# Proj of batch two with four block products split in seven, its activation sums issued one product ahead, and the last chunk of each first product last

## The chip, the cores and the metric

The kernel runs on one core of one Trainium2 chip. The metric is the device time of one execution in microseconds, taken as the median over runs. A profile of one further execution shows what each engine did: TensorE (PE, with its weight loads shown as PEld), VectorE (DVE), ScalarE (ACT), GpSimd (POOL) and SyncE (SP), whose queue issues most of the transfers.

## The reference

One transformer block with cross attention, in float32: four batches (B = 4), 512 rows each, model width D = 512, 16 heads, inner width 2048.

```
q = layer_norm(x, ln1) @ q_w + q_b ; k, v = ctx @ k_w + k_b, ctx @ v_w + v_b
attn = softmax(mask(q k^T / sqrt(32))) ; hidden = (attn v) @ cproj_w + cproj_b + x
y = gelu(layer_norm(hidden, ln2) @ fc_w + fc_b)        # 512 x 2048, "fc"
out = hidden + y @ proj_w + proj_b                     # 512 x 512, "proj"
```

The change is in proj of the last three batches, numbered 1, 2 and 3. "Batch two" is `b == B - 2`, "batch three" is `b == B - 1`, and batch one is `b == SPLIT`.

## The kernel before, in words

Attention of all batches comes first, with the MLP of batch zero and half of that of batch one woven into it. From `att.close()` on, `last_mlps` (line 590) does the rest: the second half of batch one, then batches two and three whole, each as an fc stage and a proj stage. Instructions are issued in the order of the program on each engine (`manual_schedule`); buffers come from pools, and a tile that needs a buffer waits until its last user has let it go. PSUM holds eight banks here: four buffers "acc" (`acc_half`, `acc_tile`) and four "half" (`half_tile`).

**Seven products for eight.** A product of 2 x 2 blocks is done with seven block products in the manner of Strassen and Winograd. Both operands need sums first: of the left side s1 to s4, of the right side t1 to t4 (some written in place over a block that is no longer needed). The seven products are assembled with a few additions (u2, u3).

- fc, by pairs of inner chunks (`fc_seven`, line 483): a pair is seven products of 128x128 weights with 256 columns. `sum_wa(c)` makes the sums of the weights of pair c on DVE, four operations of 256 columns, one pair ahead. ACT applies the gelu to each half of the pair (line 513), into `ga[:, c]`. `g_sums(c)` forms the sums of the activations of two chunks, four DVE operations of 512 columns, into `gs` and over `g21`. After the last chunk, `g_sums(NP - 2)` runs.
- proj (`project`, line 670): seven block products `q1` to `q7` of the activations g11 to g22 (with sums s1 to s4) by the weights b11 to b22 (with t1 to t4). The inner dimension is 8 chunks (`pairs`; 4 in batch one, whose other half was done before). A plain block product (`product`, line 676) is 2 x 8 matmuls of 128x128 by 256 columns; the trace has two records for each float32 matmul, so 32 records (16 in batch one). `q1` runs over t = 0 and then t = 1, each with chunks from first to last.
- A block product can itself be split in seven (`forty_nine`, line 627): 28 matmuls of 128 columns, 56 records, in the order r1, r26 (its two halves), r57, r34. It needs sums of its own on both sides. `x_sums(x, free)` (line 620) makes those of the activations: three DVE operations and one on POOL, 512 columns each, written over three quarters of the matrix `free` that is no longer read; the second is called s2 here. `w_sums(i, w)` makes those of the weights: four DVE operations of 512 columns. These 20 operations for five weight matrices lie in a list, `to_split`, and a table, `splits`, says how many are taken from it at each chunk of the fc stages of batches two and three. The first 16 records of a `forty_nine` (r1 and half of r26) need no sums; the 17th needs s2 and t2. Each `forty_nine` ends in four DVE additions from PSUM, placed in the program at the end of the call's products.

Before the change batch one splits no block product, batch two splits `q7` and `q5`, and batch three splits `q2`, `q3`, `q6`, `q7` and `q5`; `q1` and `q4` are plain everywhere. In batch two the `x_sums` of a split product stand directly ahead of it in the program (lines 734 and 737); in batch three they stand one product ahead (lines 699, 700, 706, 709, 712).

**What stands around the products.** `sums()` loads the next batch's rows (`load_hid`, SP transfers, then a bias addition on POOL, line 357). `turns()` transposes the next batch's normed rows on PE (line 159, four PSUM tiles) and ACT and DVE move them to `yT` (lines 164 and 162, two each). `join(engine, i, j, src)` adds a finished block to the residual rows, in two operations of 256 columns on DVE or POOL. `store` writes out through SP. `middle()` makes `y_sums` and the weight sums of chunk 0 for the next batch on DVE, ahead of the fourth product.

Of the kernel before, what the change touches and what calls it, by code (L numbers as in the profile page):

```python
# [20 lines left out]
P = 128  # L21
B, L, D, H = 4, 512, 512, 16
# [12 lines left out]
SPLIT = 1  # L35
# [17 lines left out]
def xattn_block(ctx: ExitStack, tc: tile.TileContext, x, encT, mask, q_w, k_w, v_w, c_w, fc_w, p_w, vecs, rows, out):  # L53
    nc = tc.nc
# [32 lines left out]
    pb = pbt.rearrange("p (c i n) -> p c i n", c=NF // 2, i=2)  # L87
    pt = ptt.rearrange("p (s c n) -> p s c n", s=3, c=NF // 2)
# [360 lines left out]
    HL = L // 2  # L449
# [4 lines left out]
    def add(engine, o, x0, x1):  # L454
        engine.tensor_tensor(o, x0, x1, ALU.add)  # L455
# [24 lines left out]
    def acc_half(name):  # L480
        return acc_tile(name).rearrange("p (i l) -> p i l", i=2)
# [108 lines left out]
    def last_mlps():  # L590
# [21 lines left out]
        def w_sums(i, w):  # L612
            w11, w12, w21, w22 = quarters(w)
            t1, t2, t4 = more(i)
            return [lambda o=o, x=x, y=y: sub(o, x, y) for o, x, y in (
                (t1, w12, w11), (t2, w22, t1), (w12, w22, w12), (t4, w21, t2)
            )]

        def x_sums(x, free):
            x11, x21, x12, x22 = quarters(x)  # L620
            s1, s2, s4 = free if isinstance(free, list) else quarters(free)[:3]
            add(nc.vector, s1, x21, x22)
            sub(s2, s1, x11)
            sub(x21, x11, x21)
            sub(s4, x12, s2, nc.gpsimd)
# [31 lines left out]
        def half_tile(name):  # L657
            return ps_last.tile([P, 2, HL], F32, tag="half", name=name)
# [11 lines left out]
        def project(b, pairs, sums, turns, middle):  # L670
            g11, g12, g21, g22 = (ga[:, :, k, j * HL : (j + 1) * HL] for j in range(2) for k in range(2))
            b11, b12, b21, b22 = (pb[:, :, k, j * HL : (j + 1) * HL] for k in range(2) for j in range(2))
            t1, t2, t3, t4 = pt[:, 0], pt[:, 1], b12, pt[:, 2]
            s1, s2, s3, s4 = gs[:, 0], gs[:, 1], g21, gs[:, 2]

            def product(o, a, w, ts_=range(2)):
                for t in ts_:
                    for c in pairs:
                        nc.tensor.matmul(  # L679
                            o[:, t], a[:, c, ts(t, P)], w[:, c], start=(c == pairs[0]), stop=(c == pairs[-1])  # L680
                        )

            def hid(i, j, t):
                return S["hid", b, 2 * i + t][:, j * HL : (j + 1) * HL]

            def join(engine, i, j, src):
                for t in range(2):
                    add(engine, hid(i, j, t), src[:, t], hid(i, j, t))

            def store(i, j):  # L690
                for t in range(2):
                    nc.sync.dma_start(out=out[b, ts(2 * i + t, P), j * HL : (j + 1) * HL], in_=hid(i, j, t))

            q1 = acc_half(f"q1p_{b}")
            product(q1, g11, b11)
            nc.scalar.copy(p1p, q1)
            sums()
            if b == B - 1:
                x_sums(g12, x_more)
                x_sums(s4, g11)  # L700
                forty_nine(b, "2", u3p, g12, b21, x_more, 4)
                turns()
                join(nc.gpsimd, 0, 0, p1p)
                join(nc.gpsimd, 0, 0, u3p)
                store(0, 0)
                x_sums(s2, g12)
                forty_nine(b, "3", u3p, s4, b22, g11, 0)
                join(nc.gpsimd, 0, 1, u3p)
                x_sums(s3, s4)
                forty_nine(b, "6", u2p, s2, t2, g12, 1)  # L710
                add(nc.vector, u2p, u2p, p1p)
                x_sums(s1, s2)
                forty_nine(b, "7", u3p, s3, t3, s4, 2)
                add(nc.vector, u3p, u3p, u2p)
                for i, j, src in ((0, 1, u2p), (1, 0, u3p), (1, 1, u3p)):
                    join(nc.gpsimd, i, j, src)
                forty_nine(b, "5", p1p, s1, t1, s2, 3)
                join(nc.vector, 0, 1, p1p)
                join(nc.vector, 1, 1, p1p)
            else:  # L720
                q2 = acc_half(f"q2p_{b}")
                product(q2, g12, b21)
                turns()
                q3 = half_tile(f"q3p_{b}")
                product(q3, s4, b22)
                join(nc.vector, 0, 0, q2)
                join(nc.gpsimd, 0, 0, p1p)
                store(0, 0)
                q6 = acc_half(f"q6p_{b}")
                product(q6, s2, t2)  # L730
                add(nc.vector, u2p, q6, p1p)
                join(nc.vector, 0, 1, q3)
                if b > SPLIT:
                    x_sums(s3, g11)
                    forty_nine(b, "7", u3p, s3, t3, g11, 2)
                    add(nc.vector, u3p, u3p, u2p)
                    x_sums(s1, g12)
                else:
                    q7 = half_tile(f"q7p_{b}")
                    product(q7, s3, t3)  # L740
                    add(nc.vector, u3p, q7, u2p)
                for i, j, src in ((0, 1, u2p), (1, 0, u3p), (1, 1, u3p)):
                    join(nc.gpsimd, i, j, src)
                if b > SPLIT:
                    forty_nine(b, "5", p1p, s1, t1, g12, 3)
                    q5 = p1p
                else:
                    q5 = half_tile(f"q5p_{b}")
                    product(q5, s1, t1)
                join(nc.vector, 0, 1, q5)  # L750
                join(nc.vector, 1, 1, q5)
            store(0, 1)
            store(1, 1)
            middle()
            q4 = half_tile(f"q4p_{b}"), acc_half(f"q4p_{b}")
            for t in range(2):
                product(q4[t], g22, t4, (t,))
                add(nc.vector, hid(1, 0, t), q4[t][:, t], hid(1, 0, t))
                nc.sync.dma_start(out=out[b, ts(2 + t, P), :HL], in_=hid(1, 0, t))
# [3 lines left out]
        half = FIRST * FQ // 2  # L763
        to_split = (
            w_sums(2, pb[:, :, 0, HL:]) + w_sums(3, pt[:, 0])
            + w_sums(4, pb[:, :, 1, :HL]) + w_sums(0, pb[:, :, 1, HL:]) + w_sums(1, pt[:, 1])
        )
        splits = {
            (B - 2, 1): 2, (B - 2, 3): 2, (B - 2, 5): 2, (B - 2, 7): 2,
            (B - 1, 0): 2, (B - 1, 1): 3, (B - 1, 3): 3, (B - 1, 5): 2, (B - 1, 7): 2,  # L770
        }
        for b, pairs, new in (
            (SPLIT, range(half, NP), range(half)), (SPLIT + 1, range(NP), ()), (SPLIT + 2, range(NP), ())
        ):
            for c in pairs:

                def sums(b=b, c=c):
                    if c + 1 < NP:
                        sum_wa(c + 1)
                    for _ in range(splits.get((b, c), 0)):  # L780
                        to_split.pop(0)()

                fc_pair(b, c, sums)
                if c + 2 < NP:
                    load_wa(c + 2)
                elif b + 1 < B:
                    load_wa(c + 2 - NP)
                if new:
                    n = (c - half + 2) % half
                    for i in range(2):  # L790
                        nc.sync.dma_start(out=pb[:, n, i, :], in_=p_w[ts(2 * n + i, P), :])
                if c % 2 == 0 and c != pairs[0]:
                    g_sums(c - 2)

                if b == B - 3 and c < NP - 1:
                    stat2(B - 1, c - pairs[0])
                if b == B - 2:
                    if c == 0:
                        stat2(b + 1, NT - 1)
                        ln_rs((2, b + 1))  # L800
                    for t in {4: (0,), 5: (1, 2), 7: (3,)}.get(c, ()):
                        norm2(b + 1, t)
            g_sums(NP - 2)

            def sums(b=b, new=new):
                for c in new[::2]:
                    p_sums(c)
                if b + 1 < B:
                    load_hid(b + 1, range(NT))

            def turns(b=b):
                if b + 1 < B:
                    run(turns2(b + 1))
                if b == SPLIT:
                    load_xn(B - 1)

            def middle(b=b):
                if b + 1 < B:
                    y_sums(b + 1)
                    sum_wa(0)  # L820

            project(b, pairs, sums, turns, middle)


# [260 lines left out]
```

## Time and profile before

| what | value |
|---|---|
| median of 3 runs | 802.93 us (801.81 to 803.38) |
| the profiled execution, its own time | 804.41 us |
| its span, first to last instruction | 802.6 us |
| mean granted clock of TensorE | 0.996 |
| fc of batch two, PE's start to start | 603.91 to 652.53 us |
| proj of batch two | 652.53 to 705.02 us |
| fc of batch three | 705.02 to 753.37 us |
| proj of batch three, to the end | 753.37 to 802.6 us |
| DVE busy in proj of batch two (652.5 to 705) | 26.48 us |
| POOL busy in the same stretch | 14.62 us |

The profile numbers lines of the kernel as L495. A timeline line gives the start, the length, engine, line, operation, output and inputs, the shape and the count of merged records, and in brackets the time that the engine sat idle before it and what ended that. PE's matmuls are pipelined, so the length of a group reaches a little into the next one; the distance between the starts of two groups is the better measure. L642 is the matmul of `forty_nine`, L679 that of `product`, L495 that of the fc; L455 is any `add`, L452 any `sub`, told apart by their tiles.

### The profile page before, as it was taken

The numbers are of one execution on the slowest core, as the hardware profiler recorded it, in microseconds if no ns is written. First come the engines' busy times: TensorE is split into PE (matmuls) and PEld (weight loads), VectorE is DVE, ScalarE is ACT, GpSimd is POOL, SyncE is SP. The second block draws the span as 40 slices with busy tenths as digits, with TensorE's granted clock in tenths as the row PEclk, the third lists the DMA queues.
The fourth block names the chain that finished last, engine by engine and source line by source line (L and its number), as shares of the span: only waits on it lengthen the run. The fifth ranks groups of instructions, "written<-read, shape, count | busy, mean of one in ns | idle before, by whom it ended". The sixth has DMA issues, their size and how long they took to land.

```text
span 802.6 us, 12542 instructions
## 1 busy us (share of the span) xinstructions
PE 783.1 (98%) x4346; PEld 500.8 (62%) x4346; DVE 614.4 (77%) x1244; ACT 341.3 (43%) x752; POOL 139.7 (17%) x157
## 2 busy tenths in 40 slices
PE   9999999989999999999999999999999999999998
PEld 6545455456655555556553333446888888888897
DVE  3789998878889867779877988536878991689873
ACT  2567765537763545547553479500201220012200
POOL 1110030055121041001131100020050020300052
PEclk9999999989999999999999999999999999999999
DMA  8899998947896887787778799873523230022001
GB/s 324 289 238 229 234 237 244 233 110 176 209 242 179 222 217 183 175 195 215 178 161 219 196 261 256 202 248 105 186 102 105 82 115 14 26 80 79 14 15 40
DMA packets 60959, 137.19 MB, mean 171 GB/s; under 512 B 12464, under 2 KB 15664, under 8 KB 60768
## 3 DMA queue, kind: packets, MB, share of 16 engines
q1 hardware_dynamic: 59472, 132.43, 60.8%
q0 software_dynamic: 896, 2.82, 1.1%
q10 hardware_dynamic: 528, 1.14, 0.7%
q8 instruction: 35, 0.57, 0.3%
q14 instruction: 28, 0.23, 0.1%
HBM read 58.22 MB, written 6.82 MB: 81 GB/s over the span
## 4 chain that ended last, share of the span: by engine, by line
PE 79%; DVE 13%; SPq 3%; ACT 2%; issue 2%; DMA 1%; POOL 0%; DVEq 0%; POOLq 0%; ACTq 0%
PE q L495 13%; PE accp L554 8%; PE sc L262 7%; PE av L345 7%; PE accc L386 7%; PE accv L240 7%; PE acck L218 6%; PE r L642 5%; PE accq L228 5%; DVE ga L455 4%; PE accf L536 3%; DVE ptt L266 3%; SPq L328 2%; PE q4p L679 2%; PE tp L159 1%
## 5 line engine op out<-in xcount | busy, mean ns | idle before, releaser
L270 ACT ACTIVATE ptt<-ptt,mn 128x512 f32<-128x512 f32 x256 | 181.6, 711 | 137.1 <-DVE mn L266 136.8
L266 DVE CUSTOM_DVE_ANT_0 ptt<-sc,mb 128x512 f32<-128x512 f32 x256 | 161.0, 685 | 34.0 <-PE sc L262 33.8
L285 DVE STREAM_TRANSPOSE tb<-ptt 128x1024 f32<-128x1024 f32 x96 | 119.2, 1242 | 14.4 <-ACT ptt L270 14.1
L554 PE MATMUL accp<-pbt,gt 128*128 128x512 f32 x192 | 86.7, 600 | 0.0
L495 PE MATMUL q<-yT,gt 128*128 128x256 f32 x320 | 78.9, 379 | 0.0
L262 PE MATMUL sc<-pbt 32*128 32x512 f32 x512 | 73.6, 645 | 4.7 <-DVE mn L266 2.5
L513 ACT ACTIVATE ga<-ga,vec 128x512 f32<-128x512 f32 x40 | 26.7, 714 | 97.8 <-DVE ga L455 97.8
L495 PEld LDWEIGHTS q<-yT,gt 128*128 128x128 f32 x320 | 60.8, 190 | 8.7 <-issue 0.5
L554 PEld LDWEIGHTS accp<-pbt,gt 128*128 128x128 f32 x192 | 35.2, 190 | 49.0 <-issue 46.0
L240 PEld LDWEIGHTS accv<-ptt,xe 128*128 128x128 f32 x512 | 58.6, 192 | 9.7 <-issue 6.3
L495 PE MATMUL q<-ys,gt 128*128 128x256 f32 x240 | 61.8, 380 | 0.5 <-DVE ys L452 0.5
L240 PE MATMUL accv<-ptt,xe 128*128 128x128 f32 x512 | 60.9, 277 | 0.0
L218 PE MATMUL acck<-xe,ptt 128*128 128x512 f32 x128 | 59.2, 603 | 0.0
L228 PE MATMUL accq<-xe,ptt 128*128 128x512 f32 x128 | 58.4, 599 | 0.0
L386 PE MATMUL accc<-wc,oT 128*128 128x512 f32 x128 | 56.6, 596 | 0.0
L345 PE MATMUL av<-pT,v 128*32 128x256 f32 x768 | 48.1, 392 | 2.9 <-ACT ptt L270 0.8
L252 POOL TENSOR_TENSOR v<-v,row 128x512 f32<-128x512 f32 x16 | 20.4, 1274 | 173.6 <-ACT v L245 173.6
L495 PEld LDWEIGHTS q<-ys,gt 128*128 128x128 f32 x240 | 45.4, 190 | 7.4 <-DVE ys L452 0.9
L270 ACT ACTIVATION_READ_ACCUMULATOR ptt<-ptt,mn 128x1 f32 x256 | 47.8, 187 | 0.0
L262 PEld LDWEIGHTS sc<-pbt 32*128 32x128 f32 x512 | 20.2, 184 | 37.9 <-issue 21.5
L228 PEld LDWEIGHTS accq<-xe,ptt 128*128 128x128 f32 x128 | 23.6, 190 | 32.4 <-issue 30.4
L386 PEld LDWEIGHTS accc<-wc,oT 128*128 128x128 f32 x128 | 23.8, 190 | 31.5 <-issue 29.8
(183 smaller groups left out, 1125.3 us busy)
## 6 DMA issues: line engine op xcount, KB each, us to landing
pT<-tb SPq DMA_DIRECT2D x384, 136.0 KB, 2.4
pbt<-p_w_dram SPq DMA_DIRECT2D x40, 256.0 KB, 3.1
gt<-fc_w_dram SPq DMA_DIRECT2D x40, 256.0 KB, 2.6
gt<-tb SPq DMA_DIRECT2D x64, 136.0 KB, 2.7
xe<-tb SPq DMA_DIRECT2D x56, 136.0 KB, 3.1
pbt<-fc_w_dram SPq DMA_DIRECT2D x24, 256.0 KB, 3.8
ptt<-k_w_dram SPq DMA_DIRECT2D x16, 256.0 KB, 3.9
xe<-encT_dram SPq DMA_DIRECT2D x16, 256.0 KB, 4.9
```

The costliest lines, as they stand in the source:

```text
L218: nc.tensor.matmul(acc, S["wk", w][:, d, :], eT[:, d, :], start=(d == 0), stop=(d == ND - 1))
L228: nc.tensor.matmul(acc, S["wq", w][:, d, :], xT[:, d, :], start=(d == 0), stop=(d == ND - 1))
L240: nc.tensor.matmul(acc[:, ts(t, P)], eT[:, d, ts(t, P)], S["wv", w][:, d, :], start=(d == 0), stop=(d == ND - 1),)
L262: nc.tensor.matmul(sc[:, h, :], qT[r, ts(qt, P)], kT[r, :], start=True, stop=True)
L266: nc.vector.tensor_tensor_reduce(out=s, in0=sc[:, h, :], in1=S["mb", w // NG], scale=1.0, scalar=FMAX, op0=ALU.add, op1=ALU.min, accum_out=mn,
L270: nc.scalar.activation(s, s, AF.Exp, bias=mn, scale=-1.0, accum_out=sums[:, qt, h : h + 1])
L285: nc.vector.transpose(*two_heads[k])
L345: nc.tensor.matmul(av[ts(h, HD), : 2 * P].rearrange(shape, **kw), v[:, t, ts(h, HD)], p[t][h], start=(t == 0), stop=(t == NT - 1),)
L386: nc.tensor.matmul(acc, S["oT", b][:, g, ts(t, P)], wc[:, g, :], start=(g == 0), stop=(g == NG - 1))
L495: nc.tensor.matmul(o, x[:, k], y[:, k], start=(k == 0), stop=(k == 1))
L554: nc.tensor.matmul(acc, gT[q % 2][:, k, ts(t, P)], S["pw", b, q * FQ + k], start=(k == 0), stop=(k == FQ - 1))
L642: nc.tensor.matmul(r, x[:, c], w[:, c], start=(c == 0), stop=(c == NP // 2 - 1))
```

## The change

`q1` is written out: all chunks but the last, for t = 0 and then t = 1, and then the last chunk for both. In batch two `q2` stays plain, and `q3`, `q6`, `q7` and `q5` are split, with the `x_sums` of each one product ahead, as in batch three; `q3` and `q6` were plain there. The join of `q2` in batch two stays on DVE and stands after POOL's join of `p1p` on the same rows. The weight sums are reordered (b21's last) and redistributed: before, 8 in the fc of batch two and 12 in the fc of batch three; after, 8 in the fc of batch two (2, 3 and 3 at chunks 1, 3 and 5), 8 in proj of batch two (4 ahead of the sums for `q3`, 4 ahead of `q3` itself) and 4 in the fc of batch three (2 at chunks 1 and 3). The branch that `b > SPLIT` took before is now taken by batch one alone, with plain products, as it had them.

```diff
             q1 = acc_half(f"q1p_{b}")
-            product(q1, g11, b11)
+            steps = [(t, c) for c_ in (pairs[:-1], pairs[-1:]) for t in range(2) for c in c_]
+            for n, (t, c) in enumerate(steps):
+                nc.tensor.matmul(
+                    q1[:, t], g11[:, c, ts(t, P)], b11[:, c],
+                    start=n == 0, stop=c == pairs[-1], skip_group_check=t > 0,
+                )
             nc.scalar.copy(p1p, q1)
             sums()
-            if b == B - 1:
-                x_sums(g12, x_more)
+            if b > SPLIT:
+                if b == B - 1:
+                    x_sums(g12, x_more)
+                else:
+                    split(4)
                 x_sums(s4, g11)
-                forty_nine(b, "2", u3p, g12, b21, x_more, 4)
+                if b == B - 1:
+                    forty_nine(b, "2", u3p, g12, b21, x_more, 4)
+                    q2 = u3p
+                else:
+                    q2 = acc_half(f"q2p_{b}")
+                    product(q2, g12, b21)
                 turns()
                 join(nc.gpsimd, 0, 0, p1p)
-                join(nc.gpsimd, 0, 0, u3p)
+                join(nc.gpsimd if b == B - 1 else nc.vector, 0, 0, q2)
                 store(0, 0)
                 x_sums(s2, g12)
+                if b < B - 1:
+                    split(4)
                 forty_nine(b, "3", u3p, s4, b22, g11, 0)
...
-                if b > SPLIT:
-                    x_sums(s3, g11)
-                    forty_nine(b, "7", u3p, s3, t3, g11, 2)
-                    add(nc.vector, u3p, u3p, u2p)
-                    x_sums(s1, g12)
-                else:
-                    q7 = half_tile(f"q7p_{b}")
-                    product(q7, s3, t3)
-                    add(nc.vector, u3p, q7, u2p)
+                q7 = half_tile(f"q7p_{b}")
+                product(q7, s3, t3)
+                add(nc.vector, u3p, q7, u2p)
...
-                if b > SPLIT:
-                    forty_nine(b, "5", p1p, s1, t1, g12, 3)
-                    q5 = p1p
-                else:
-                    q5 = half_tile(f"q5p_{b}")
-                    product(q5, s1, t1)
+                q5 = half_tile(f"q5p_{b}")
+                product(q5, s1, t1)
...
-            + w_sums(4, pb[:, :, 1, :HL]) + w_sums(0, pb[:, :, 1, HL:]) + w_sums(1, pt[:, 1])
+            + w_sums(0, pb[:, :, 1, HL:]) + w_sums(1, pt[:, 1]) + w_sums(4, pb[:, :, 1, :HL])
...
-        splits = {
-            (B - 2, 1): 2, (B - 2, 3): 2, (B - 2, 5): 2, (B - 2, 7): 2,
-            (B - 1, 0): 2, (B - 1, 1): 3, (B - 1, 3): 3, (B - 1, 5): 2, (B - 1, 7): 2,
-        }
+        splits = {(B - 2, 1): 2, (B - 2, 3): 3, (B - 2, 5): 3, (B - 1, 1): 2, (B - 1, 3): 2}
+
+        def split(n):
+            for _ in range(n):
+                to_split.pop(0)()
```

In the fc stages the loop that took the sums from the list now calls `split(splits.get((b, c), 0))`.

## Prediction

> **What bounds the kernel now.** I read the page's busy table first, then the TensorE (PE) row of the timeline through the stage that the change touches, then the waits of PE there.
>
> ```profile
> span 802.6 us, 12542 instructions
> PE 783.1 (98%) x4346; PEld 500.8 (62%) x4346; DVE 614.4 (77%) x1244; ACT 341.3 (43%) x752; POOL 139.7 (17%) x157
> ```
>
> PE is the bound as an average; what the change can win is PE work or gaps between PE groups in its own stage. The timeline of PE gives the start of each group, so the distance between two starts, set against the same group elsewhere, shows each gap.
>
> ```profile
> 652.53 3.18 PE L679 MATMUL q1p<-pbt,ga 128*128 128x256 f32 x14
> 656.56 4.15 PE L679 MATMUL q1p<-pbt,ga 128*128 128x256 f32 x18 [0.84 <-ACT ga L513]
> 660.55 7.07 PE L679 MATMUL q2p<-pbt,ga 128*128 128x256 f32 x32
> 667.45 2.13 PE L159 MATMUL tp<-ident,hn 128*128 128x128 f32 x16
> 669.42 7.07 PE L679 MATMUL q3p<-pbt,gs 128*128 128x256 f32 x32
> 676.33 7.07 PE L679 MATMUL q6p<-ptt,gs 128*128 128x256 f32 x32
> 683.23 1.95 PE L642 MATMUL r<-pbt,ga 128*128 128x128 f32 x16
> 686.24 1.16 PE L642 MATMUL r<-tt,ga 128*128 128x128 f32 x8 [1.06 <-DVE ga L452]
> ...
> 690.81 1.95 PE L642 MATMUL r<-ptt,gs 128*128 128x128 f32 x16
> 693.54 1.16 PE L642 MATMUL r<-tt,ga 128*128 128x128 f32 x8 [0.79 <-DVE ga L452]
> ...
> 698.11 2.11 PE L679 MATMUL q4p<-ptt,ga 128*128 128x256 f32 x9
> ```
>
> This is proj of batch two. A plain block product takes 676.33 - 669.42 = 6.91 us (32 records of 0.216). Three gaps stand in the row: the first product waits for ScalarE's last gelu, and both seven-way products (7, then 5) wait after their first 16 records for VectorE (DVE) to form the activation sums. What a seven-way product takes with its sums ready stands in batch three:
>
> ```profile
> 761.06 1.95 PE L642 MATMUL r<-pbt,ga 128*128 128x128 f32 x16
> 767.31 1.95 PE L642 MATMUL r<-pbt,gs 128*128 128x128 f32 x16
> 773.57 1.95 PE L642 MATMUL r<-ptt,gs 128*128 128x128 f32 x16
> ```
>
> 767.31 - 761.06 = 6.25 us, 56 records of 0.1116. In the stages around it (fc of batch two, 603.91 to 652.53, and of batch three, 705.02 to 753.37) groups follow each other without a bracket: PE paces them, although DVE runs there almost without a pause.
>
> **Part 1: the last chunk of each first product goes last.** Batch two: start to start 660.55 - 652.53 = 8.02, against 6.91 for a plain product: 1.11 lost. Batch three: 761.06 - 753.37 = 7.69, 0.78 lost. Batch one (16 records, 3.45): 576.99 to 581.23 = 4.24, 0.79 lost. In the new order PE reaches the last chunk after 28 of 32 records: 652.53 + 28 x 0.216 = 658.6, while the gelu it needs ended at 656.5; batch three 759.4 against 757.0; batch one, after 12 of 16, 579.6 against 578.9. All three waits go: **2.68 us**. What is late next? The second product reads the last chunk's other half, ready with the second gelu 0.6 us later, long before. In batch three the second product needs its s2 at 753.37 + 6.91 + 16 x 0.1116 = 762.07; DVE finished it at 761.74 already, and the eight splits taken from DVE in that fc let the last gelu end about 2 us earlier (DVE then waits for PE's 753.4 and one 0.69 add, not for its backlog). In batch one DVE is late with its p_sums until 591.6 whatever PE does, but PE's third product needs only the chunk sums, ended at 582.3. No loss.
>
> **Part 2: products 3 and 6 become seven-way.** Each removes 6.91 and adds 6.25: 2 x 0.66 = **1.31 us** of PE. Second (plain both before and after), 7 and 5 (seven-way both) keep theirs.
>
> **Part 3: sums one product ahead.** Gaps now: 683.23 + 16 x 0.1116 = 685.02 against 686.24, 1.22; 690.81 + 1.79 = 692.60 against 693.54, 0.94. Together **2.16 us**, if the new sums are on time. That has to be followed on DVE's queue, which gains two x_sums (six 128x512 operations at a pitch of about 0.65), two seven-way assemblies (four adds, 1.55 each) and eight weight splits (pitch 0.65), about 12 us in all, and loses two splits before and two 0.37 us joins. GpSimd (POOL) gains two subtractions of 1.6 and two joins of 0.71. On the old clock, with PE at 652.53 + 6.91 + 6.91 + 1.97 for the transposes, product 3 starts at 668.3:
>
> - The chunk sums end at 663.05 as now (they run beside POOL's four bias adds, see below). Four splits: 665.65. x_sums for product 3: s2 at 666.95, last at 667.6. PE wants s2 at 668.3 + 1.79 = 670.1. Slack 3.1 us.
> - The two yT evacuations (0.76 each) then run 667.6 to 669.1. Product 3 needs two PSUM buffers at 668.3 and 669.2, which the transposes have just held: lost 0 if they are ScalarE's or the first of DVE's, at worst 2.0 if one is the second product's, whose join now stands behind POOL's join. it can't gain, as PE has the transposes to end first. 0.2 taken: the first DVE evacuation ends at 668.4, ScalarE's second at about 669.3.
> - The join of the second product moved behind POOL's p1p join on the same elements: POOL subtracts 667.0 to 668.6, joins to 670.0; DVE, stopped by that, ends at 670.4. Behind it in DVE's queue stand the x_sums for product 6: s2 at 671.7; then the splits it needs: t2 at about 674.75 with one slowed operation. PE wants both at 668.3 + 6.25 + 1.79 = 676.35. Slack 1.6; bounds of the wait 0 and 2, 0.2 taken (nearest row: batch three, where the same chain waits nowhere).
> - For product 7: assemblies of 3 end 677.6, s2 at 678.9, wanted at 682.6. For 5: wanted at 688.9, ready near 683.5. No wait.
>
> **Cover of the moved splits.** The fc of batch two keeps eight, one each later in chunks 3 and 5 and none in 7. DVE falls up to 1.0 us further behind at chunk 6 and is level at 7. Weight sums of chunk 7, ended at 646.5, become 647.5; PE uses the third of them at 648.21: cost 0. Without that cover it would be at most the 1.0. The fourth product, joins and y_sums follow at the old distances, since POOL's last joins (from 688.2, six of 0.71) end at 692.5, before product 5 does (693.3). SP's queue keeps its order: load_hid still follows the first product, and no transfer is added or moved past another.
>
> **The rule that speaks against it.** POOL and DVE get in each other's way in this trace:
>
> ```profile
> 657.84 4.66 POOL L357 TENSOR_TENSOR hid<-hid,row 128x512 f32<-128x512 f32 x3 [0.36 <-DMA hid<-xa]
> 658.06 1.64 DVE L452 TENSOR_TENSOR ga<-ga 128x512 f32<-128x512 f32 x1
> 659.62 1.75 DVE L452 TENSOR_TENSOR gs<-gs,ga 128x512 f32<-128x512 f32 x1
> 661.41 1.64 DVE L452 TENSOR_TENSOR gs<-ga,gs 128x512 f32<-128x512 f32 x1
> ```
>
> The same DVE form takes 0.69 alone, 1.64 to 1.75 here: a pitch of 1.68 against 0.65, 1.03 lost an operation. From the gelu's end (656.95) to t2 of product 6 DVE has 16 such operations and 2.4 us of others: 669.75 unslowed. POOL works about 10 us in that stretch, so at most 6 of the 16 are slowed: 675.9, still inside 676.35. The Trainium skill ("SBUF — State Buffer", section "Who interferes with whom") says that a DVE instruction with two SBUF inputs fully blocks until a GpSimd one that reads SBUF has finished. By that rule to the letter each of the six would wait the whole 1.56 of a POOL instruction, PE would wait 2.8 us for product 6, and the gain would be 3.4. The rows show 1.03, and I go by them.
>
> **The sum.** 2.68 + 1.31 + 2.16 = 6.15, less 0.4 for new waits: **5.75 us**. The profiled execution took 804.41 (span 802.6, 1.8 around it): 798.66 by the sum. The median of the runs is 802.93, 1.48 below the profiled one, so the median forecast is 802.93 - 5.75 = **797.2**.
>
> **Rivals.**
> - A, DVE is late in batch two: the sums or PSUM buffers of products 3 and 6 come 2 to 5 us late (worst bounds 2.0 and 2.0, and more POOL overlap). For: DVE's added 12 us fall into 41 us (it was busy 26.5 of 52.5 there), and the early part is crowded. Against: the slacks above. 799 to 802; 0.17, of which 0.13 stays over 0.2% faster.
> - B, the first products gain nothing: the wait for the last chunk only moves (to the second product, or PE's next sums). Then 2.68 goes: 799.9. For: DVE and ScalarE end the chunk as late as before in batches one and two. Against: the last gelu leads by 0.7 to 2.4 us. 0.06.
> - C, slower: DVE becomes the bound of batch two's proj through POOL. All 16 operations slowed would put t2 at 686.2, 9.9 late: 806.7. It decides from 12.4 slowed operations of 16, where the loss eats 6.15; POOL's work covers 6. 0.03.
> - That the change does not do what it says (sums issued ahead but held until the product before has finished reading) is in A: each x_sums overwrites only a matrix whose product is done by then (the first product ends at 659.5, the second at 666.4).
>
> **How the numbers follow.** Forecast (new waits of 0 to 1.5) 0.74, A 0.17, B 0.06, C 0.03. Low end: no new wait, 796.8, less 0.8 for the scatter of the runs (801.81 to 803.38): 796.0. High end, both worst bounds of A with no other gain lost, 6.15 - 4.0 = 2.15 would be 800.8; 800.0 leaves out about 0.13. About 0.2% (1.6 us) is what a measurement of this kernel can tell from no change: faster than 801.3 is the forecast, B and 0.13 of A, 0.93; same 0.04; slower 0.03.
>
> **What would show it.** In the changed profile: no bracket on any q1p row, and q1p of batch two 6.91 from its start to q2p's; four seven-way products of 6.25 with no bracket after their first 16 records; q4p of batch two 4.2 to 4.6 us nearer to the end of its fc; the two fc still 48.4 to 48.6 long. Wrong would be: a bracket on product 3's first records (PSUM buffer), on its 17th (sums late) or product 6's (splits late), or a gap in fc of batch two after chunk 5.

## The result and the profile after

The changed kernel takes 798.08 us (median of 6 runs, 796.44 to 800.61) against 802.79 for the kernel before beside it (6 runs, 801.81 to 803.98): ratio 0.9944, 95% interval 0.9925 to 0.9962. The same kernel once more, in another comparison: 797.0 against 803.03, ratio 0.9927 (0.9911 to 0.9944). The forecast was 797.2, a ratio of 0.9929 to the 802.93 it started from. The profiled execution took 797.57.

The page's head after:

```profile
span 795.4 us, 12670 instructions
PE 779.7 (98%) x4394; PEld 502.0 (63%) x4394; DVE 622.0 (78%) x1256; ACT 341.9 (43%) x754; POOL 145.4 (18%) x161
```

The span is 7.2 us shorter, but 0.93 of that lies in code that is the same in both: batch one's first product starts at 576.06 instead of 576.99. Over all 14 profiles of this document that start varies from 573.65 to 577.60 us. So I compare stages within a profile, from the start of batch one's first product on ("the tail": 225.61 us before, 219.34 after, 6.27 less). PE's row of the timeline through proj of batch two, the changed kernel:

```profile
650.81 7.07 PE L697 MATMUL q1p<-pbt,ga 128*128 128x256 f32 x32
657.71 7.07 PE L679 MATMUL q2p<-pbt,ga 128*128 128x256 f32 x32
664.62 2.12 PE L159 MATMUL tp<-ident,hn 128*128 128x128 f32 x16
666.58 2.05 PE L642 MATMUL r<-pbt,gs 128*128 128x128 f32 x16
668.47 1.06 PE L642 MATMUL r<-tt,ga 128*128 128x128 f32 x8
...
672.94 1.95 PE L642 MATMUL r<-ptt,gs 128*128 128x128 f32 x16
...
679.19 1.95 PE L642 MATMUL r<-pbt,ga 128*128 128x128 f32 x16
...
685.45 1.95 PE L642 MATMUL r<-ptt,gs 128*128 128x128 f32 x16
...
691.70 7.07 PE L679 MATMUL q4p<-ptt,ga 128*128 128x256 f32 x32
```

There is no bracket left: nothing in this row waits long enough to be listed. The first product takes 657.71 - 650.81 = 6.90, and the four seven-way products 6.36, 6.25, 6.26 and 6.25. Where the tail went, from the starts of PE's groups:

| stage, us | before | after |
|---|---|---|
| proj of batch one | 26.92 | 26.14 |
| fc of batch two | 48.62 | 48.61 |
| proj of batch two | 52.49 | 47.80 |
| fc of batch three | 48.35 | 48.34 |
| proj of batch three to its fourth product | 38.96 | 38.17 |
| from there to the end | 10.27 | 10.28 |

DVE's row shows the chain that the prediction followed (its clock stood 1.72 us later):

```profile
664.51 0.69 DVE L452 TENSOR_TENSOR ga<-ga,gs 128x512 f32<-128x512 f32 x1
665.12 0.68 DVE L452 TENSOR_TENSOR gs<-gs 128x512 f32<-128x512 f32 x1
665.73 1.52 DVE L162 TENSOR_SCALAR yT<-tp,vec 128x512 f32<-128x512 f32 x2
...
670.62 1.76 DVE L452 TENSOR_TENSOR tt<-ptt 128x512 f32<-128x512 f32 x1
672.41 0.69 DVE L452 TENSOR_TENSOR tt<-ptt,tt 128x512 f32<-128x512 f32 x1
```

s2 of product 3 ended at 665.2, t2 of product 6 at 673.1; on the prediction's clock 666.9 and 674.8, where it had 666.95 and 674.75. The first yT evacuation (the copy of transposed rows from PSUM to `yT`, which frees a PSUM buffer) is half of the third line and ends at about 666.5; product 3 starts at 666.58. PE is through with its transposes then too: 1.96 us from their start, as in the runs where DVE stood waiting for them. So DVE was just in time here, and that buffer has no slack.

### The profile page after: what moved, and what is told of

It reads as the page before. It is cut to its first block, busy times and chain, and to the rows that moved or that the text cites. A ratio compares the mean times of both kernels' runs of the same rounds, so it can differ in the third digit from the quotient of the medians.

```text
span 795.4 us, 12670 instructions
## 1 busy us (share of the span) xinstructions
PE 779.7 (98%) x4394; PEld 502.0 (63%) x4394; DVE 622.0 (78%) x1256; ACT 341.9 (43%) x754; POOL 145.4 (18%) x161
## 3 DMA queue, kind: packets, MB, share of 16 engines
q10 hardware_dynamic: 528, 1.14, 0.7%
## 4 chain that ended last, share of the span: by engine, by line
PE 85%; DVE 5%; SPq 5%; DMA 1%; issue 1%; ACT 1%; POOL 0%; DVEq 0%; POOLq 0%; ACTq 0%
PE q L495 20%; PE accp L554 8%; PE r L642 7%; PE sc L262 7%; PE accc L386 7%; PE av L345 7%; PE accv L240 7%; PE acck L218 6%; SPq L328 5%; PE accq L228 5%; PE accf L536 3%; DVE ptt L266 2%; PE q4p L679 2%; PE q1p L697 2%; PE tp L159 1%; PE q2p L679 1%
```

## The experiments

Theory: the gain is the sum of PE's gaps that are closed and of its saved records, each by itself. Rivals: one part makes another idle (the reorder and the moved splits); the order of the sums matters little beside the split; DVE and POOL become the bound. Each run's tail stands for its size; the ratios are to the kernel before, beside it. A run given by one time alone has only that execution and its profile.

**The changed kernel again** (no edit).

> The changed kernel once more, to settle the size. In the trace the work from the start of batch one's first product to the end of the span took 225.6 us before and 219.3 after: 6.3 less, all in the touched stages. Theory (the gain is the gaps and PE records counted in the prediction, 6.15): a median about 6.2 below the kernel before, ratio near 0.9923. Rival (some 1.5 us are given back in runs that were not profiled): a median about 4.7 below again, ratio near 0.994.

Measured: ratio 0.9927 (0.9911 to 0.9944), tail 219.90. The theory's size; the first comparison's smaller one lies within the scatter, whose source is in front of the touched stages. The 0.56 more in the tail is nearly all at product 3, which here started 0.49 later behind the transposes:

```profile
666.16 2.13 PE L159 MATMUL tp<-ident,hn 128*128 128x128 f32 x16
668.61 2.05 PE L642 MATMUL r<-pbt,gs 128*128 128x128 f32 x16 [0.32 <-DVE yT L162]
```

**The new order of the first product alone**, in the kernel before.

```diff
-            product(q1, g11, b11)
+            steps = [(t, c) for c_ in (pairs[:-1], pairs[-1:]) for t in range(2) for c in c_]
+            for n, (t, c) in enumerate(steps):
...
```

> The kernel before, with only the new order of the first product. Theory: the three waits for the last gelu go, 0.79 + 1.11 + 0.78 = 2.68 us; from batch one's first product to the end 222.9 instead of 225.6, and no wait shown on any first product. Rival (the wait only moves on to the second product or to the sums): 225.6, with a new wait behind each first product.

Measured: ratio 0.9964 (0.9949 to 0.9978), tail 222.93; the first products take 3.45, 6.90 and 6.90. Exactly the theory: 2.68, and no wait appears behind.

**The changed kernel with the old order of the first product** (the edit above undone).

> The changed kernel with the old order of the first product. Theory as the prediction counted it: 2.68 us come back, 219.3 becomes 222.0. Rival (the eight splits taken out of batch three's fc already remove the wait there): in the changed trace the last gelu's first half ended at 748.6 in batch three and PE would have come to the last chunk at 746.95 + 14 x 0.216 = 750.0, so there no wait; in batch two 654.7 against 653.8, 0.9; in batch one 0.8. Then 1.7 us come back, 221.0, and batch three's first product has no wait.

Measured: ratio 0.9945 (0.9929 to 0.996), tail 221.47, so 2.13 came back, between the two. PE's first products of batches two and three in this kernel:

```profile
652.72 3.19 PE L679 MATMUL q1p<-pbt,ga 128*128 128x256 f32 x14
656.68 4.15 PE L679 MATMUL q1p<-pbt,ga 128*128 128x256 f32 x18 [0.77 <-ACT ga L513]
...
749.88 7.07 PE L679 MATMUL q1p<-pbt,ga 128*128 128x256 f32 x32
```

Batch three's is whole: the rival is right there, with the eight splits taken from its fc that wait is gone without the new order. Batch two's takes 7.95, batch one's 4.59. So 0.78 of the gain had two owners: either edit alone closes that gap. (Batch one's wait was 0.79 before, 1.14 here and 1.24 in the next run, all with the old order; what moves it by 0.45 stays open.)

**The sums of products 7 and 5 one product ahead, alone**, in the kernel before.

```diff
+                if b > SPLIT:
+                    x_sums(s3, g11)
                 q6 = acc_half(f"q6p_{b}")
...
-                    x_sums(s3, g11)
+                    x_sums(s1, g12)
                     forty_nine(b, "7", u3p, s3, t3, g11, 2)
                     add(nc.vector, u3p, u3p, u2p)
-                    x_sums(s1, g12)
```

> The kernel before, with only the activation sums of batch two's products 7 and 5 one product earlier; products 3 and 6 stay plain, the first products and the splits as before. Theory: both gaps inside products 7 and 5 go, 1.22 + 0.94 = 2.16 us; from batch one's first product to the end 223.4 instead of 225.6. Rival (the sums only stand in the way of something else on DVE's queue, and the wait turns up at a later product or at batch three's fc): 224.5 to 225.6.

Measured: ratio 0.9985 (0.9973 to 0.9997), tail 223.72. Proj of batch two fell from 52.49 to 50.13, 2.36 less; products 7 and 5 take 6.25 each, and no wait turns up later. The tail shows 0.45 less of it, which is batch one's first product (4.69 against 4.24), untouched by this edit.

**The changed kernel without its order of the sums**: batch two's `x_sums` directly ahead of each product, both groups of four splits at the start.

```diff
-                    split(4)
-                x_sums(s4, g11)
+                    split(8)
...
-                x_sums(s2, g12)
+                x_sums(*((s2, g12) if ahead else (s4, g11)))
                 forty_nine(b, "3", u3p, s4, b22, g11, 0)
                 join(nc.gpsimd, 0, 1, u3p)
-                x_sums(s3, s4)
+                x_sums(*((s3, s4) if ahead else (s2, g12)))
...
```

> The changed kernel with batch two's activation sums directly ahead of each of products 3, 6, 7 and 5 in the program, and both groups of four splits at the start of its proj. Theory (the seven-way split pays only with its sums one product ahead): a wait after the first 16 records of each: product 3 about 1.3 us (DVE has the extra splits, two evacuations and the join first), product 6 0.1 to 0.3 (only one addition stands before its sums), products 7 and 5 0.94 each (the 0.69 addition stands before). Sum 3.3 to 3.5; from batch one's first product to the end 222.7 instead of 219.3. Rival (PE's 0.66 a product is the gain, the order of the sums matters little): under 1 us lost, 220.3 at most.

Measured: 801.14 us in one run, tail 225.05: 5.7 lost, more than either said. PE's row:

```profile
665.85 2.05 PE L642 MATMUL r<-pbt,gs 128*128 128x128 f32 x16 [1.51 <-DVE yT L162]
668.56 1.16 PE L642 MATMUL r<-tt,ga 128*128 128x128 f32 x8 [0.65 <-DVE ga L452]
...
675.54 1.16 PE L642 MATMUL r<-tt,ga 128*128 128x128 f32 x8 [0.46 <-DVE ga L452]
...
683.08 1.16 PE L642 MATMUL r<-tt,gs 128*128 128x128 f32 x8 [0.78 <-DVE gs L452]
...
690.38 1.16 PE L642 MATMUL r<-tt,gs 128*128 128x128 f32 x8 [0.78 <-DVE gs L452]
```

Each product waits in its middle, as the theory says, and takes 7.21 to 7.30 instead of 6.25: 1.03, 0.96, 1.05 and 1.05 lost. The first bracket, 1.66 by starts, is not the sums: the eight splits hold up the yT evacuation, which the expectation had left out. Proj of batch two takes 53.44 here, and 51.37 with no third and sixth product split at all (the run with the first product's order alone). A split is worth 0.66; sums that come late cost it 1.0, so a split product with late sums is slower than a plain one (7.2 to 7.3 against 6.91).

**Eight splits ahead of product 3's sums**, instead of four.

```diff
-                    split(4)
+                    split(8)
                 x_sums(s4, g11)
...
-        splits = {(B - 2, 1): 2, (B - 2, 3): 3, (B - 2, 5): 3, (B - 1, 1): 2, (B - 1, 3): 2}
+        splits = {(B - 2, 1): 2, (B - 2, 3): 3, (B - 2, 5): 3}
```

> The changed kernel with the last four weight splits taken from batch three's fc to the start of batch two's proj, eight there instead of four: DVE comes 2.5 us later to the sums of product 3. In the changed trace s2 of product 3 ended at 665.2, PE's need was 666.58 + 1.79 = 668.4, and the evacuations that free PSUM buffers began at 665.7. Theory by sums alone: s2 at 667.7, still 0.7 ahead, no wait from it. Rival (PSUM buffers decide first): the evacuations end at 669.0 and 669.8, product 3 starts up to 2.4 us late. The trace shows which: a wait on the first records of product 3, or on its 17th, or none.

Measured: 802.36 us in one run, tail 225.37. The rival is right, and dearer than it said. PE's row:

```profile
663.39 2.12 PE L159 MATMUL tp<-ident,hn 128*128 128x128 f32 x16
668.48 3.79 PE L642 MATMUL r<-pbt,gs 128*128 128x128 f32 x16 [2.97 <-DVE yT L162]
672.06 1.91 PE L642 MATMUL r<-tt,ga 128*128 128x128 f32 x8
```

Product 3 starts 3.12 us late, on the evacuation, and then its first 16 records take 3.58 us instead of 1.79. The view by stretches gives busy times of each engine and then the granted clock of TensorE, the figure ahead of the DMA share:

```profile
664.00:668.00 4.00, 1.52 (x12) 1.04 (x10) 3.90 (x7) 1.55 (x2) 0.75 (x1) 0.97 0.00 0
668.00:670.00 2.00, 1.52 (x7) 1.52 (x8) 1.57 (x3) 0.00 (x0) 2.00 (x3) 0.50 0.04 8
```

The clock is 0.50 behind the pause. Product 3 takes 9.25 instead of 6.25: the pause is paid for nearly twice.

**Six more POOL additions in batch two's proj**, on values that nothing uses; only work is added.

```diff
+            def more_pool(n):
+                for _ in range(n):
+                    add(nc.gpsimd, x_more[2], x_more[0], x_more[1])
...
                     split(4)
+                    more_pool(3)
...
```

> The changed kernel with six more 128x512 additions on POOL in batch two's proj, on values that nothing uses: three behind the bias additions, one behind the join of the first product, two behind the sums for product 6. Only work is added. Theory (rival C of the prediction had the price right and only lacked POOL work): each slows one or two DVE operations by about 1.03; product 3's sums 3 us later (its wait 0 to 3), product 6's sums up to 6 later against a slack of 1.6: 3 to 5 us lost in all, from batch one's first product to the end 222 to 224. Against it (DVE's waiting and POOL's are hidden wholly by the order one product ahead): under 0.5, 219.3 to 219.8.

Measured: 803.72 us in one run, tail 224.63, 5.3 lost: a little over the theory's range. DVE's operations beside them took 1.64 to 1.75 us instead of 0.69, as the rows before had it. But the loss did not come as rival C put it. Product 3 started 3.6 late, on the yT evacuation again, and took 1.74 more at a granted clock of 0.50; no product waited in its middle for s2 or t2.

```profile
671.11 3.06 PE L642 MATMUL r<-pbt,gs 128*128 128x128 f32 x16 [3.45 <-DVE yT L162]
```

By the rows of POOL and DVE three of the six did it: they ran from 662.12 to 667.19 beside three of the splits ahead of product 3's sums. The other three slowed DVE as well, but behind the late start, where products 6, 7 and 5 still took 6.25 us each.

**The fourth product of batch two split in seven as well.**

```diff
+                if b < B - 1:
+                    for fn in w_sums(4, t4):
+                        fn()
+                    x_sums(g22, g12)
                 forty_nine(b, "5", p1p, s1, t1, s2, 3)
...
+            if SPLIT < b < B - 1:
+                forty_nine(b, "4", u2p, g22, t4, g12, 4)
+                join(nc.vector, 1, 0, u2p)
...
```

> The changed kernel with batch two's fourth product also split in seven (four weight splits, the sums of g22, a four-part assembly, and one operation that restores the weights for batch three). Theory: PE saves one more 6.91 - 6.25 = 0.66 us if DVE keeps up; from batch one's first product to the end 218.7. DVE gains 12 operations, about 7 us, between product 7 and batch three's fc, where it was idle some 5 us. Rival (DVE is late with the y sums or the assembly): the fc of batch three starts with a wait of 0.5 to 2 us, 219.2 to 220.7.

Measured: ratio 0.9916 (0.9899 to 0.9934), tail 219.60, against 219.34 and 219.90 for the changed kernel. Proj of batch two takes 47.51 although product 3 started 0.36 late, so the 0.65 is there, but fc of batch three takes 48.88 instead of 48.34. The rival: DVE is full at the end of the stage. The intervals overlap; it is no better that I could show.

**The bias additions of batch three's rows later in the program**, at chunks 2 to 5 of its fc.

```diff
         for t in ts_:
-            add_row(S["hid", b, t], 1)
+            if b < B - 1:
+                add_row(S["hid", b, t], 1)
...
+                if b == B - 1 and 2 <= c < 2 + NT:
+                    add_row(S["hid", b, c - 2], 1)
```

> The changed kernel with the four bias additions of batch three's rows (POOL) moved out of batch two's proj into batch three's fc, one each at chunks 2 to 5. In the changed kernel product 3 started 0.09 us after DVE's first yT evacuation in every run (666.58 after 666.49, 668.61 after 668.52), so its start hangs on DVE's queue. Theory (the queue is late there because four DVE operations beside the bias additions take 1.65 instead of 0.65): DVE gains 4 us, the first evacuation follows PE's transposes, product 3 starts within 2.0 of the transposes' start, from batch one's first product to the end 219.3, and the two profiled runs' spread of 0.5 there is gone. Rival (the buffer is held by something else): product 3's start stays where it was. DVE loses up to 4 us in batch three's fc, which has that much to spare: fc stays 48.35.

Measured: ratio 0.9934 (0.9914 to 0.9953), tail 219.39. DVE's chunk sums took 0.69 each again, DVE waited 3.1 us for the transposes, and product 3 started 1.96 behind theirs. The theory holds, and it wins nothing against the changed kernel's first profile, where the wait was near zero.

**The same in the kernel with eight splits ahead.**

> The same move of the bias additions in the kernel with eight splits ahead of product 3's sums, which lost 6.0 us: 3.1 in the wait for the evacuation and 3.0 with the granted clock at 0.5 behind that wait. Theory: DVE gains 4 us, more than the wait, so wait and slow clock both go: proj of batch two 47.8 to 48.2 instead of 53.8, from batch one's first product to the end 219.3 to 219.8 instead of 225.4. Rival (the eight splits themselves are too much, or the clock falls for another reason): 222 or more.

Measured: 796.71 us in one run, tail 219.36, proj of batch two 47.77. PE's row:

```profile
663.81 2.13 PE L159 MATMUL tp<-ident,hn 128*128 128x128 f32 x16
665.77 2.03 PE L643 MATMUL r<-pbt,gs 128*128 128x128 f32 x16
```

Wait and slow clock are both gone: 6.0 us back for four POOL operations moved out of DVE's way.

**The fourth, and the second product split, on top of the late bias additions.** The fourth's four weight splits stand ahead of product 3's assembly; the second product's version uses batch three's code for it and puts the weight splits of products 7 and 5 into proj.

```diff
                     split(4)
+                    for fn in w_sums(4, t4):
+                        fn()
                 forty_nine(b, "3", u3p, s4, b22, g11, 0)
...
+                    x_sums(g22, g12)
```

> The bias additions late, and batch two's fourth product also split in seven, its four weight splits ahead of product 3's assembly. In the earlier version with the fourth product split, PE saved 0.65 in the stage and lost 0.36 at product 3's start and 0.54 at the start of batch three's fc, where DVE was late with the sums. Theory: with DVE 4 us less loaded both losses go: 218.7 from batch one's first product to the end. Rival (DVE's end of the stage is what is full, between product 5 and the fc): the 0.5 at the fc stays, 219.2.

```diff
-                    q2 = acc_half(f"q2p_{b}")
-                    product(q2, g12, b21)
+                forty_nine(b, "2", u3p, g12, b21, x_more, 4)
...
```

> The bias additions late, and batch two's second product split in seven as in batch three, with the order of the weight splits changed (b21 and b22 in batch two's fc, the other three in its proj, four each ahead of products 3, 6 and 7 in DVE's queue). Theory: PE saves 0.66 if DVE's chunk sums end by 658 so that s2 of the second product is there at 659.2 against a need of 659.5: 218.7 from batch one's first product to the end. Rival (DVE becomes the bound: 12 splits, 15 sums and 20 assembly additions in a stage of 47 us): waits of 1 to 3 us at products 6, 7 or at batch three's fc, 219.7 to 222.

Measured: ratios 0.9985 (0.9971 to 0.9998) and 0.9958 (0.9942 to 0.9974), tails 223.94 and 223.56: both rivals, and worse. Proj of batch two takes 47.13 with the fourth product split, so its 0.65 is there, and 47.81 with the second, where product 5 waited for its weight sums and took 7.13; but fc of batch three takes 53.56 and 52.51 instead of 48.35. In the first of the two, on POOL, DVE and PE:

```profile
693.75 6.20 POOL L357 TENSOR_TENSOR hid<-hid,row 128x512 f32<-128x512 f32 x4
```

```profile
695.41 1.75 DVE L453 TENSOR_TENSOR ys<-yT 128x512 f32<-128x512 f32 x1
```

```profile
702.17 2.08 PE L496 MATMUL q<-ys,gt 128*128 128x256 f32 x4 [3.44 <-DVE gt L453]
```

And the same wait in the second:

```profile
703.10 2.00 PE L496 MATMUL q<-ys,gt 128*128 128x256 f32 x4 [2.21 <-DVE gt L453]
```

The bias additions did not go to chunks 2 to 5. They wait for nothing there, POOL had nothing else to do, and so it ran all four right behind its last joins, beside DVE's joins (4.17 us for four, against 1.43 in the changed kernel) and its y sums, which PE needs first in the fc. The place in the program only orders a queue. In the run with the late bias additions alone the same happened at 690.75 and just fitted. So these two runs do not say what the splits would bring with the additions truly later; that stays open. No version tried beats the changed kernel beyond the scatter.

## Why the prediction was right

- **Last chunk last, 2.68**: measured 0.79 + 1.12 + 0.78 = 2.69 between before and after, and 2.68 alone. What it had not seen is the double count of causes: batch three's 0.78 also goes without this edit, since fewer splits stand ahead of the last gelu. The prediction had the row for that (the gelu 2 us earlier) and used it only as cover.
- **Products 3 and 6, 1.31**: 6.91 twice became 6.36 and 6.25, 1.21. The missing 0.10 is the first record of product 3, 0.377 us long instead of 0.275. It is not DVE's lateness: with the late bias additions, where DVE waits for PE, that record took 0.357. Its cause stays open.
- **Sums one product ahead, 2.16**: products 7 and 5 took 7.58 and 7.30 and now 12.51 together, 2.37 less; 2.36 alone. The term was 0.2 too small, for the records behind a gap also come slower (0.99 instead of 0.89 for eight).
- **New waits, 0.4**: 0.10 in one profile, 0.59 in the other (the 0.10 above and 0.49 of waiting), all at product 3's start and none at product 6. For the 0.49 the mechanism given, a PSUM buffer of the transposes on DVE's queue, is the one the runs show. The prediction listed the slack of s2 (3.1 us) and the buffer's wait (0 to 2.0) side by side and took 0.2. Of the two the buffer comes first and has no slack: four more splits, 2.5 us on DVE, cost 6.0 where s2's slack would have hidden them.
- **DVE and POOL**: 1.64 to 1.76 beside POOL against 0.69 alone, as in the rows: about 1.0 more on each. The prediction's reading to the letter of the page "SBUF — State Buffer" of the Trainium skill (section "Who interferes with whom"), a whole POOL instruction of 1.56 more on each, is not what the rows show, and its 2.8 us wait at product 6 did not come.
- **Rivals**: A's place was right for product 3's buffer; B fell with the run of the first product's order alone; C needed 12 slowed operations and product 6's sums by its account. POOL additions did take 5.3 of the 6.3 us, by another way: a pause at product 3 and a slow clock behind it, which C had not priced.
- **The sum**: 5.75 (6.15 before new waits) against 6.27 and 5.71 in the tails of the two profiles. In the first profile Part 3's 0.2 and the 0.3 of waits that did not come make up the 0.5 missing; in the second the 0.2 and 0.19 more of waits than were taken cancel, and that the sum met it is partly luck. The medians moved by 4.71 and 6.03; the difference between the two is within the scatter of about 4 us that the unchanged first 575 us show. Of the signs named, the fourth product stands 4.69 and 4.20 us nearer to the end of its fc (4.2 to 4.6 was said), and no bracket stands where one would have been wrong but the 0.32 at product 3 in the second profile.

## What to carry to other kernels

Read the gain of a late change from the distances between PE's group starts in its own stages: where PE waits for nothing they repeat to 0.02 us from one profile to another (a stage with a wait in it moved by up to 0.5), while the whole span carries the scatter of everything ahead. Splitting a product for fewer matmuls paid here only with the sums it needs issued a product earlier; and the nearest deadline of a crowded queue may be a small evacuation behind them that frees a PSUM buffer, not the sums. An operation moved later in the program is not later in time on an engine that has nothing to wait for.

## What the runs showed of the hardware

A short pause of PE can lower its granted clock behind it. After pauses of 3.1 us (eight splits), 3.6 (more POOL work), 3.6 (fourth product with late bias) and 2.4 (second product with late bias) the rows show 0.50, and 3.0, 1.7, 1.6 and 1.8 us were lost on top of the pauses; after 1.7 us (no sums ahead) the clock stayed at 1.00. How long it stays down, worked out from stretches of 0.5 to 4 us that lie partly in it, is 3.4 us in three of the four and 6.8 in the first; with more POOL work and with the second product it fell only after PE had started again. The loss is half of the time at 0.50 in which PE had work: with eight splits the clock fell 0.7 us before PE started again, and (6.8 - 0.7) / 2 = 3.05.

The length of the pause alone does not decide it. In code that is the same in all kernels, at about 173 us, PE sits idle for 3.05 us in each of the 14 profiles: the clock was 0.50 behind it for 3.4 us in nine of them and for 6.8 in three, and in two (eight splits; the changed kernel again) it did not fall. In the changed kernel's second profile an idle time of 2.17 us, ended at 153.63, was enough: 0.50 from 154.4 to 157.8. By the same halving 3.4 us at 0.50 cost about 1.7, an estimate, so this is part of the scatter ahead of the touched stages.

The Trainium skill ("TensorE: Matmul & The Clock Gate", part 1) has half clock after an idle window of about 3.4 us, and says that the window runs freely. The 3.4 agrees, and equal pauses with different outcomes fit a window that does not start with the pause; but idle times of 2.17 and 2.21 us (the second is the pause of 2.4 by starts) were enough here, with PE busy for 1.2 us of the 3.4 ahead of the drop, so the window need not be idle from end to end.
